# A GNN and attention kernel whose beginning was reordered: x loaded ahead of the weights, q of the first group by plain products, later norms and transposes among its products

## Chip, cores, metric

One core of a Trainium2 chip. The metric is the device time of one execution in microseconds (us), median of several. The profile's span, about 1.8 us shorter, is that of one profiled execution. The granted clock is TensorE's, as a share of its full speed, as the profile gives it.

## The reference

Input x is 128 batches of 128 rows of 512, float32. Layer 0 adds to each row one number from adj times the normed x. Layer 1 is masked attention with 8 heads.

```python
h = jnp.maximum(_layernorm(x, axis=-1), 0.0)
x = x + _L0_gnn_ref(h, adj, adj, L0_gnn_b)   # a row maximum of adj @ h + b, clipped at 0
h = jnp.maximum(_layernorm(x, axis=-1), 0.0)
q = (x @ Wq + bq); k = (x @ Wk + bk); v = (x @ Wv + bv)   # of this h
scores = einsum(q, k) / 8 + mask(adj == 0); weights = softmax(scores)
x = x + einsum(weights, v)
```

Layer 0 adds a constant per row, which the second norm takes out again. So both layers share one normed h, and the kernel norms each batch once.

## The kernel before

A group is four batches. For each batch: `norm` (statistics on VectorE, `rstd` on POOL), `norm_end` (h on VectorE, scaled on ScalarE; POOL adds bv to x for the output), transposes on TensorE (the first two groups only), and `adjacency` (TensorE product, maximum on VectorE). For each group and each of q, k, v there are seven fast products p1 to p7 (a Strassen scheme) of sums of h and of the weight, in place of eight. Cuts are marked with `...`.

```python
ps_mm = ctx.enter_context(tc.tile_pool(name="ps_mm", bufs=4, space=PSUM))
ps_sc = ctx.enter_context(tc.tile_pool(name="ps_sc", bufs=1, space=PSUM))
ps_av = ctx.enter_context(tc.tile_pool(name="ps_av", bufs=1, space=PSUM))
...
nc.scalar.dma_start(adj_sb, adj)
load(0)                                        # x of batches 0-3, two pieces, on SP's queue
for name, src in (("q", wq), ("k", wk), ("v", wv)):
    nc.scalar.dma_start(W[name], src.rearrange("(c p) f -> p c f", p=P))
nc.gpsimd.dma_start(b0_sb, ...)                # then bq, bk, bv on POOL's queue
...
def norm_end(m):
    g, i = divmod(m, G)
    nc.vector.tensor_scalar(HN[m], X[g][:, i, :], MV[m][:, 0:1], 0.0, op0=ALU.subtract, op1=ALU.max)
    nc.scalar.activation(HN[m], HN[m], AF.Copy, scale=RSTD[m])
    nc.gpsimd.tensor_tensor(X[g][:, i, :], X[g][:, i, :], bv_sb, op=ALU.add)
...
for g in (0, 1):
    for m in range(g * G, g * G + G + 1):
        if m < g * G + G:
            norm(m); norm_end(m)
        if m > g * G:
            transposes(m - 1); adjacency(m - 1)
    for k in range(4):
        h_sum(g, k)                            # VectorE
    if g == 0:
        weight_sums(nc.vector, "q"); weight_sums(nc.gpsimd, "k"); weight_sums(nc.gpsimd, "v")
        PR[0] = q, k, v = [Products(0, n) for n in "qkv"]
        for p in (q.p1, q.p6, q.p2, ..., v.p5, v.p4):
            p()
for m in (2 * G, 2 * G + 1):
    norm(m); norm_end(m); blocks(m); adjacency(m)
...
for b in range(B):                             # the loop: scores, products of the next group, output
    ...
```

The instructions are issued on each engine in the order written.

## Time and profile before

| | before |
|---|---|
| median time | 1646.46 us (1645.5 to 1647.39, 4 runs) |
| span of the profiled run | 1643.9 us |
| TensorE, VectorE, ScalarE, POOL busy | 97%, 68%, 26%, 16% |
| first scores (start of the loop) | 95.51 us |
| from there to the end | 1548.4 us |

I call the start of the first scores T. It is the first TensorE instruction that writes the tile `sc` from `qT` and `kT` in the timeline. From there TensorE has no gap until its last batches.

### The profile page before, as it was taken

To read this page: it belongs to the slowest core of one execution; us is meant where nothing else is said; L and a number is where in the kernel's file an instruction comes from. 1 tells how busy PE (TensorE), PEld (TensorE's weight loads), DVE (VectorE), ACT (ScalarE), POOL (GpSimd) and SP (SyncE) were. 2 spreads that over 40 slices of the span, in tenths; PEclk is the share of its full clock that TensorE was granted. 3 is DMA by queue.
4 is the path that set the end of the run, shared out by engine and by line. 5 is a ranking of instruction groups with operands and counts; after the bars stand their busy time and mean duration, and the time that the engine had idled before them with its cause. 6 is when DMAs were issued, how large, how long until landed. Compare 5 with 4: busy or idle time off the path is not lost.

```text
span 1643.9 us, 29453 instructions
## 1 busy us (share of the span) xinstructions
PE 1593.4 (97%) x11811; PEld 1326.5 (81%) x11811; DVE 1124.6 (68%) x2050; ACT 421.3 (26%) x841; POOL 262.4 (16%) x278
## 2 busy tenths in 40 slices
PE   4879999999999999999999999999999999999996
PEld 3658888888888888888888888888888888888885
DVE  5467676677776677776677777677777677777655
ACT  2222222222222222222222222222222222222221
POOL 5111111111111111111111111111111111111000
PEclk8989999999999999999999999999999999999998
DMA  4022223322223322223322223322223322123201
GB/s 161 1 49 49 65 66 77 69 68 48 62 71 73 69 69 50 61 71 71 71 68 54 56 70 71 70 69 65 45 69 71 72 69 67 42 69 72 52 20 40
DMA packets 299003, 104.02 MB, mean 63 GB/s; under 512 B 264369, under 2 KB 264497, under 8 KB 298865
## 3 DMA queue, kind: packets, MB, share of 16 engines
q1 hardware_dynamic: 296960, 98.64, 24.9%
q10 hardware_dynamic: 1728, 3.21, 0.6%
q8 instruction: 94, 1.54, 0.4%
q0 software_dynamic: 176, 0.27, 0.1%
q14 instruction: 45, 0.36, 0.1%
HBM read 37.03 MB, written 33.55 MB: 43 GB/s over the span
## 4 chain that ended last, share of the span: by engine, by line
PE 94%; issue 3%; DVE 1%; POOL 1%; ACT 0%; DMA 0%; DVEq 0%; POOLq 0%
PE mm L357 70%; PE sc L442 9%; PE pav L464 9%; PE mm L298 7%; DMA xg<-in_x_dram 0%; DVE w L455 0%; POOL rstd L257 0%; DVE st L252 0%; PE mm L292 0%; ACT hn L265 0%; DVE amax L299 0%; DVE hs L316 0%; POOL xg L266 0%; POOL sk_sb L325 0%; POOL sv_sb L323 0%
## 5 line engine op out<-in xcount | busy, mean ns | idle before, releaser
L257 POOL TENSOR_TENSOR rstd<-ve,mhalf 128x1 f32<-128x1 f32 x128 | 84.6, 661 | 1246.3 <-DVE ve L255 1216.7
L450 ACT ACTIVATE w<-sc 128x512 f32<-128x512 f32 x256 | 138.9, 595 | 518.3 <-PE sc L442 518.3
L464 PEld LDWEIGHTS pav<-v,w 128*64 128x64 f32 x4096 | 131.1, 138 | 99.9 <-issue 54.8
L357 PE MATMUL mm<-hs,sq_sb 128*128 128x256 f32 x768 | 186.2, 386 | 8.9 <-DVE sq_sb L324 8.9
L357 PE MATMUL mm<-sv_sb,hs 128*128 128x256 f32 x768 | 176.3, 379 | 0.0
L357 PE MATMUL mm<-hs,sk_sb 128*128 128x256 f32 x768 | 176.2, 379 | 0.0
L357 PEld LDWEIGHTS mm<-hs,sq_sb 128*128 128x128 f32 x768 | 144.6, 192 | 31.3 <-issue 9.2
L266 POOL TENSOR_TENSOR xg<-xg,bv_sb 128x512 f32<-128x512 f32 x128 | 162.7, 1271 | 33.4 <-DVE hn L262 26.9
L455 DVE TENSOR_TENSOR w<-w,live 128x512 f32<-128x512 f32 x256 | 164.7, 685 | 3.2 <-ACT w L450 3.2
L265 ACT ACTIVATE hn<-hn,rstd 128x512 f32<-128x512 f32 x128 | 92.9, 725 | 273.5 <-DVE hn L262 202.3
L357 PEld LDWEIGHTS mm<-sv_sb,hs 128*128 128x128 f32 x768 | 146.2, 190 | 19.6
L357 PEld LDWEIGHTS mm<-hs,sk_sb 128*128 128x128 f32 x768 | 146.2, 190 | 19.6
L464 PE MATMUL pav<-v,w 128*64 128x65 f32 x4096 | 149.4, 225 | 6.9 <-DVE w L455 6.9
L442 PE MATMUL sc<-qT,kT 64*128 64x128 f32 x2048 | 151.1, 288 | 0.0
L298 PE MATMUL mm<-hn,adjT 128*128 128x512 f32 x256 | 137.0, 618 | 9.6 <-ACT hn L265 9.6
L405 DVE TENSOR_TENSOR u<-mm,p1b 128x512 f32<-128x512 f32 x64 | 44.3, 692 | 132.4 <-PE mm L357 132.4
L442 PEld LDWEIGHTS sc<-qT,kT 64*128 64x128 f32 x2048 | 126.4, 190 | 10.3 <-issue 1.5
L357 PE MATMUL mm<-hT,wk_sb 128*128 128x256 f32 x512 | 124.2, 386 | 0.0
L357 PE MATMUL mm<-hT,wq_sb 128*128 128x256 f32 x512 | 124.2, 386 | 0.0
L299 DVE TENSOR_REDUCE amax<-mm 128x1 f32<-128x512 f32 x128 | 86.1, 673 | 54.7 <-PE mm L298 54.1
L357 PE MATMUL mm<-wv_sb,hT 128*128 128x256 f32 x512 | 121.0, 379 | 0.0
L357 PEld LDWEIGHTS mm<-wv_sb,hT 128*128 128x128 f32 x512 | 97.5, 190 | 13.0
(81 smaller groups left out, 2026.8 us busy)
## 6 DMA issues: line engine op xcount, KB each, us to landing
xg<-in_x_dram SPq DMA_DIRECT2D x64, 512.0 KB, 5.2
out_dram<-o SPq DMA_DIRECT2D x128, 256.0 KB, 2.1
hT<-tb SPq DMA_DIRECT2D x960, 32.0 KB, 2.0
wq_sb<-in_L_gnn_Wq_dram ACTq DMA_DIRECT2D x1, 1024.0 KB, 11.4
wk_sb<-in_L_gnn_Wk_dram ACTq DMA_DIRECT2D x1, 1024.0 KB, 16.2
wv_sb<-in_L_gnn_Wv_dram ACTq DMA_DIRECT2D x1, 1024.0 KB, 18.6
bv_sb<-in_L_gnn_bv_dram POOLq DMA_DIRECT2D x1, 256.0 KB, 8.7
adj_sb<-in_adj_dram ACTq DMA_DIRECT2D x1, 64.0 KB, 3.3
```

Of the source, the lines that this page charges most:

```text
L257: nc.gpsimd.tensor_tensor(rstd, ve, mhalf, op=ALU.pow)
L265: nc.scalar.activation(HN[m], HN[m], AF.Copy, scale=RSTD[m])
L266: nc.gpsimd.tensor_tensor(X[g][:, i, :], X[g][:, i, :], bv_sb, op=ALU.add)
L298: nc.tensor.matmul(pa, adjT, HN[m], start=True, stop=True)
L299: nc.vector.reduce_max(AMAX[g][:, i : i + 1], pa, axis=AX.X)
L357: nc.tensor.matmul(bank[:, r, :], lhs, rhs, start=first and r == 0 and c == 0, stop=r == 1 and c == 1, skip_group_check=True,)
L405: nc.vector.tensor_tensor(self.u3, self.b, self.pf[1], op=ALU.add)
L442: nc.tensor.matmul(psc[:, j, f, :], KT[g][r, f, i * D : (i + 1) * D], QT[g][r, f, i * D : (i + 1) * D], start=True, stop=True,)
L450: nc.scalar.activation(w[:, j], psc[:, j], AF.Exp, scale=HD ** -0.5)
L455: nc.vector.tensor_tensor(w[:, j], w[:, j], live_h, op=ALU.mult)
L464: nc.tensor.matmul(pav[r, h // 4, (h % 4) * HE : (h % 4 + 1) * HE], w[:, h % 2, h // 2, r], V[g % 2][:, i, h, :], start=True, stop=True,)
```

## The change

The intent: let TensorE start earlier and keep it fed until the loop. (1) x comes ahead of the weights, over two queues. (2) q of group 0 by plain products, which need no sums; VectorE makes the sums of k meanwhile, and POOL those of v (those of q, for the later groups, follow among the products). (3) Norms, transposes and adjacency of batches 4 to 9 stand among the products of k and v. Transposes now use the buffer of the scores and early adjacency that of the output, each of which exists once, and one small copy goes from VectorE to ScalarE.

```diff
-        load(0)
+        X[0] = xpool.tile([P, G, N], F32, name="xg")
+        for i in range(G):
+            (nc.sync, nc.scalar)[i % 2].dma_start(X[0][:, i, :], x[i])
         for name, src in (("q", wq), ("k", wk), ("v", wv)):
-            nc.scalar.dma_start(W[name], src.rearrange("(c p) f -> p c f", p=P))
+            for h in range(2):
+                (nc.sync, nc.scalar)[h].dma_start(W[name][:, 2 * h : 2 * h + 2, :], ...)
...
+        def plain_q(t):
...
+            for f in range(2):
+                bank = ps_mm.tile([P, 2, HT2], F32, name="mm")
+                for r in range(2):
+                    k = 2 * f + r
+                    for c in range(NC):
+                        nc.tensor.matmul(bank[:, r, :], W["q"][:, c, k * P : (k + 1) * P], h[:, :, c], ...)
+                    nc.scalar.activation(QT[0][:, k, ...], bank[:, r], AF.Identity, bias=bq_sb[:, k : k + 1])
...
+            for m in range(G):
+                norm(m)
+                norm_end(m)
+                if m > 0:
+                    early(m - 1)            # transposes and adjacency
+            plain_q(0)
+            early(G - 1)
+            weight_sums(nc.vector, "k")
+            for k in range(4):
+                h_sum(0, k)
+            plain_q(1)
+            weight_sums(nc.gpsimd, "v")
+            for s, p in enumerate((k.p1, k.p6, k.p2, k.p7, k.p5, k.p4, v.p1, k.p3, v.p6, v.p2, v.p7, v.p5, v.p4)):
+                p()
+                m = G + s // 2
+                if m < 2 * G + 2:
+                    if s % 2 == 0:
+                        norm(m)
+                        norm_end(m)
+                    elif m < 2 * G:
+                        early(m)
+                    else:
+                        blocks(m)
+                        adjacency(m, ...)
...
```

More of the change, by code (lines that the diff above doesn't have):

```diff
@@ L219, in fast @@
         nc.scalar.dma_start(adj_sb, adj)
-        load(0)
+        X[0] = xpool.tile([P, G, N], F32, name="xg")
+        for i in range(G):
+            (nc.sync, nc.scalar)[i % 2].dma_start(X[0][:, i, :], x[i])
         for name, src in (("q", wq), ("k", wk), ("v", wv)):
-            nc.scalar.dma_start(W[name], src.rearrange("(c p) f -> p c f", p=P))
+            for h in range(2):
+                (nc.sync, nc.scalar)[h].dma_start(
+                    W[name][:, 2 * h : 2 * h + 2, :],
+                    src[2 * h * P : (2 * h + 2) * P].rearrange("(c p) f -> p c f", p=P),
+                )
         nc.gpsimd.dma_start(b0_sb, b0.rearrange("(p o) -> p o", o=1))
@@ L237, in fast @@
         nc.tensor.transpose(pt[:, :D], adj_sb, ident)
-        nc.vector.tensor_copy(adjT, pt[:, :D])
+        nc.scalar.copy(adjT, pt[:, :D])
         nc.vector.tensor_single_scalar(live, adjT, 0.0, op=ALU.not_equal)
@@ L289, in transposes, with adjacency @@
             g, i = divmod(m, G)
-            ph = ps_mm.tile([P, NC, D], F32, name="mm")
+            ph = ps_sc.tile([P, 2, NC, D], F32, name="sc")
             for c in range(NC):
-                nc.tensor.transpose(ph[:, c], HN[m][:, c * P : (c + 1) * P], ident)
-            nc.scalar.copy(HT[g][:, i], ph)
-        def adjacency(m):
+                nc.tensor.transpose(ph[:, 0, c], HN[m][:, c * P : (c + 1) * P], ident)
+            nc.scalar.copy(HT[g][:, i], ph[:, 0])
+        def adjacency(m, pa=None):
             g, i = divmod(m, G)
-            pa = ps_mm.tile([P, 512], F32, name="mm")
+            if pa is None:
+                pa = ps_mm.tile([P, 512], F32, name="mm")
             nc.tensor.matmul(pa, adjT, HN[m], start=True, stop=True)
@@ L316, in h_sum, with weight_sum @@
             nc.vector.tensor_sub(HB[g][o], HB[g][a], HB[g][b])
-        def weight_sums(eng, n):
-            w = W[n]
-            a11, a21 = w[:, 0:2, 0:HT2], w[:, 0:2, HT2:N]
-            a12, a22 = w[:, 2:4, 0:HT2], w[:, 2:4, HT2:N]
-            s1, s2, s3, s4 = (WS[n][:, k] for k in range(4))
-            eng.tensor_tensor(s1, a21, a22, op=ALU.add)
-            eng.tensor_tensor(s2, s1, a11, op=ALU.subtract)
-            eng.tensor_tensor(s3, a11, a21, op=ALU.subtract)
-            eng.tensor_tensor(s4, a12, s2, op=ALU.subtract)
-            WA[n] = dict(a11=a11, a12=a12, a22=a22, s1=s1, s2=s2, s3=s3, s4=s4)
+        def weight_sum(eng, n, k):
+            if k == 0:
+                w = W[n]
+                WA[n] = dict(
+                    a11=w[:, 0:2, 0:HT2], a21=w[:, 0:2, HT2:N],
+                    a12=w[:, 2:4, 0:HT2], a22=w[:, 2:4, HT2:N],
+                    **{f"s{j + 1}": WS[n][:, j] for j in range(4)},
+                )
+            o, a, op, b = ("s1 a21 + a22", "s2 s1 - a11", "s3 a11 - a21", "s4 a12 - s2")[k].split()
+            eng.tensor_tensor(
+                WA[n][o], WA[n][a], WA[n][b], op=ALU.add if op == "+" else ALU.subtract
+            )
+        def weight_sums(eng, n):
+            for k in range(4):
+                weight_sum(eng, n, k)
         class Products:
@@ L418, in p3 @@
                 self.add(self.dst(0, 1), self.c, self.u2)
+        def plain_q(t):
+            if t == 0:
+                QT[0] = proj.tile([P, NC, T], F32, name="qT")
+            h = HT[0][:, 2 * t : 2 * t + 2]
+            for f in range(2):
[3 more added lines that the diff above has]
+                    for c in range(NC):
+                        nc.tensor.matmul(
+                            bank[:, r, :], W["q"][:, c, k * P : (k + 1) * P], h[:, :, c],
+                            start=r == 0 and c == 0, stop=r == 1 and c == NC - 1,
+                            skip_group_check=True,
+                        )
+                    nc.scalar.activation(
+                        QT[0][:, k, t * HT2 : (t + 1) * HT2], bank[:, r], AF.Identity,
+                        bias=bq_sb[:, k : k + 1],
+                    )
         def products(g):
@@ L482, in fast, with early @@
         with tc.manual_schedule():
-            for g in (0, 1):
-                for m in range(g * G, g * G + G + 1):
-                    if m < g * G + G:
+            def early(m):
+                transposes(m)
+                adjacency(m, ps_av.tile([P, 2, 512], F32, name="pav")[:, 0])
+            for m in range(G):
[6 more added lines that the diff above has]
+            weight_sums(nc.vector, "k")
+            for k in range(4):
+                h_sum(0, k)
+            plain_q(1)
+            weight_sums(nc.gpsimd, "v")
+            _, k, v = PR[0] = [None] + [Products(0, n) for n in "kv"]
+            for s, p in enumerate((
+                k.p1, k.p6, k.p2, k.p7, k.p5, k.p4, v.p1, k.p3, v.p6, v.p2, v.p7, v.p5, v.p4,
+            )):
+                p()
+                m = G + s // 2
+                if m < 2 * G + 2:
+                    if s % 2 == 0:
                         norm(m)
                         norm_end(m)
-                    if m > g * G:
-                        transposes(m - 1)
-                        adjacency(m - 1)
-                for k in range(4):
-                    h_sum(g, k)
-                if g == 0:
-                    weight_sums(nc.vector, "q")
-                    weight_sums(nc.gpsimd, "k")
-                    weight_sums(nc.gpsimd, "v")
-                    PR[0] = q, k, v = [Products(0, n) for n in "qkv"]
-                    for p in (
-                        q.p1, q.p6, q.p2, q.p7, q.p5, q.p4, k.p1, k.p6, q.p3, k.p2, k.p7,
-                        k.p5, k.p4, v.p1, k.p3, v.p6, v.p2, v.p7, v.p5, v.p4,
-                    ):
-                        p()
-            for m in (2 * G, 2 * G + 1):
-                norm(m)
-                norm_end(m)
-                blocks(m)
-                adjacency(m)
+                    elif m < 2 * G:
+                        early(m)
+                    else:
+                        blocks(m)
+                        adjacency(m, ps_av.tile([P, 2, 512], F32, name="pav")[:, 0])
+                if s >= 4 and s % 2 == 0 and s < 12:
+                    weight_sum(nc.gpsimd, "q", s // 2 - 2)
+                if s >= 8 and s < 12:
+                    h_sum(1, s - 8)
             move(2 * G + 1)
```

## The prediction

> **What bounds the kernel now.** I read the page's busy shares and slices first, then the busy times by stretch, then the timeline of the first 100 us engine by engine, then the chain of waits there. TensorE is busy 97% of the span, and the slice row is full from the seventh slice on. What the page calls low is the beginning, and the change touches only that.
>
> ```profile
> PE   4879999999999999999999999999999999999996
> PEclk8989999999999999999999999999999999999998
> ```
>
> A slice is 41 us, so some 30 to 40 us of TensorE time are missing in the first 100 us, besides the end, which the change leaves alone. The stretches tell where (columns: length, busy us of PE, PEld, DVE, ACT, POOL with counts, granted clock, DMA share, GB/s):
>
> ```profile
> 8.40:21.50 13.10, 8.04 (x23) 4.13 (x24) 4.94 (x12) 4.04 (x8) 7.18 (x8) 0.87 0.98 352
> 21.50:32.90 11.40, 2.55 (x11) 1.57 (x9) 10.45 (x9) 2.13 (x5) 11.24 (x8) 0.84 0.01 3
> 32.90:65.40 32.50, 32.50 (x144) 28.40 (x145) 10.41 (x14) 4.42 (x10) 0.96 (x1) 0.95 0.00 1
> 65.40:95.50 30.10, 15.02 (x38) 7.04 (x36) 17.41 (x38) 6.34 (x10) 11.44 (x12) 0.69 0.00 1
> ```
>
> There are two holes. From 21.5 to 32.9 TensorE waits for VectorE, which makes the operand sums of the first fast product. From 65.4 to 95.5 it waits for the norms of batches 4 to 9, at a mean clock of 0.69. The timeline has the instructions (start, us, engine, line, idle before and its releaser):
>
> ```profile
> 12.30 1.26 POOL L266 TENSOR_TENSOR xg<-xg,bv_sb 128x512 f32<-128x512 f32 x1 [5.14 <-issue]
> 13.52 0.73 POOL L257 TENSOR_TENSOR rstd<-ve,mhalf 128x1 f32<-128x1 f32 x1
> 20.01 0.72 ACT L265 ACTIVATE hn<-hn,rstd 128x512 f32<-128x512 f32 x1 [2.79 <-POOL rstd L257]
> 22.14 1.89 PE L357 MATMUL mm<-hT,wq_sb 128*128 128x256 f32 x8
> 32.88 3.53 PE L357 MATMUL mm<-hs,sq_sb 128*128 128x256 f32 x8 [8.85 <-DVE sq_sb L324]
> 43.16 1.89 PE L357 MATMUL mm<-hT,wk_sb 128*128 128x256 f32 x8
> 93.50 2.07 PE L298 MATMUL mm<-hn,adjT 128*128 128x512 f32 x2 [3.42 <-ACT hn L265]
> 95.51 2.08 PE L442 MATMUL sc<-qT,kT 64*128 64x128 f32 x16
> ```
>
> At 95.51 the loop over batches begins and TensorE then runs without gaps at about 11 us a batch. So the change is worth the shift of that one time. I call it T; it is 95.5 now.
>
> **What the Trainium skill says.** (1) "TensorE: Matmul & The Clock Gate", Part 1: the array runs at half rate until it has been busy for a window of about 3.4 us. The trace agrees: the eight instructions at 32.88, after 8.85 us of idleness, take 3.53 us, the same eight at 43.16 take 1.89. (2) The same page, under engine queue depths: ACT, DVE and GpSimd run strictly in order. The trace agrees: rstd of batch 1 on POOL waits behind the addition of bv to batch 0, and that addition waits for bv, which landed 8.7 us after its issue at 3.50, so at 12.2. (3) "DMA: Bandwidth & Descriptors", Issuing engines are not separate DMA queues: transfers from all issuers interleave on the same 16 engines. The trace agrees: share 0.98 at 352 GB/s with two queues active, so splitting x over two queues adds no bandwidth. (4) "SBUF — State Buffer", SBUF: two separate sides: a VectorE instruction with two inputs in SBUF and a GpSimd one that reads it exclude each other. The trace agrees: a 128x512 sum on VectorE takes 0.68 us alone, but starts at 1.64 to 1.75 us intervals while POOL makes weight sums, and POOL's go from 1.27 to 1.7.
>
> **Part one: x first.** x of batch 0 lands some 1 us earlier than the 5.22 us of now (256 KB on each of two queues in place of 512 KB beside a weight). It buys nothing: POOL holds rstd of batch 1 until bv is there. Transfers from POOL's queue take turns with the two others, as before; smaller pieces of x ahead of it may bring bv earlier by up to 2 us. I take 0.5 us.
>
> **Part two: the first four batches.** Transposes go to a buffer that exists once (of the scores) and adjacency to another (of the output), where four were free before. So transposes of batch 1 wait for the copy of batch 0, which stands behind hn of batch 1 on ACT: 14.3 + 0.7 + 0.5 = 15.5 in place of 15.06. Adjacency of batch 2 waits for amax of batch 1. Cost about 0.5 us, which cancels the gain of part one. So hn of batch 3 is at about 20.5, transposes and adjacency of batch 2 end at about 20.
>
> **Part three: q by plain products.** Each half is 16 products of 128x256, which the trace will show as 32 instructions (the 4 that make up one fast product show as x8). A fast product starts every 1.727 us (mean of 43.16 to 60.42, ten of them), so a half is 4 x 1.727 = 6.9 us and both are 13.8. Seven fast products of q took 12.1, so this is 1.7 us more TensorE work. But the first half starts at 20 with no sums, and the second follows batch 3's transposes and adjacency (1.36 us, from 20.78 to 22.14): 20.0 + 6.9 + 1.4 + 6.9 = 35.2. During it VectorE makes 4 k sums and 4 h sums from about 29 on. POOL's v sums start at 21.2 and need about 4 x 1.3 us, so they are over; VectorE needs 8 x 0.65 = 5.2 us and is ready at 34.5. The hole of 21.5 to 32.9 is gone.
>
> **Part four: norms among the products.** From 35.2 on: 13 products x 1.727 = 22.5 us, four pairs of transposes and adjacency x 1.36 = 5.4, two adjacencies x 0.86 (the steady loop, 106.42 to 107.28) = 1.7. Sum 29.6, end 64.8 if no gap is left. There are gaps. The order of instructions shows each batch's norm on VectorE behind amax of the batch before it, and in three of six steps (6, 8, 9) also behind a sum that reads a product just finished. From the end of what VectorE reads, TensorE waits for: [the sum 0.7 +] statistics 0.7 + mean 0.2 + ve 0.2, rstd on POOL 0.7, hn on ACT 0.7, with 0.02 to 0.1 between engines. Worked through by step:
> - batch 4: hn stands on ACT behind the four bias copies of the first product (1.5 us): gap 0.75
> - batches 5 and 7: chain from adjacency to hn 3.45 us, beside two products of 3.45: gap 0 to 0.1 each
> - batches 6, 8, 9: sum, norm, rstd, hn from the end of the first product of the step is 0.2 + 3.2, beside one product of 1.73: gap 1.7 each
> Together 0.75 + 0.1 + 3 x 1.7 = 5.95 us. T = 64.8 + 5.9 = 70.7.
>
> **The sum.** 95.5 - 70.7 = 24.8. The first scores also no longer start cold: 16 instructions took 2.01 us on the chain where a later batch took 1.09, so 0.9 more. 25.7 us, or 1.56% of 1646.0: 1620.3. I predict 1620.
>
> **Rivals.**
> - *The gaps among the products are not there* (VectorE and ACT run ahead further than I think). Then T is 65 and the time 1614. For: DVE is busy only 10.4 of 32.5 us beside the products now. Against: its instructions run in order, and the sums stand ahead of the norms.
> - *The early chain moves too*: bv lands at 9, hn of batch 3 comes 3 us earlier, and the time is 1617. With the first rival 1611, the only way I see to more than 2%. For: the transfers ahead of bv are smaller. Against: the engines are as full as before, and stats of batch 2 wait for amax of batch 0 at 11.4 anyway.
> - *New waits*: single buffers and gaps push TensorE under the busy share that keeps its clock up, so products among the norms run at half rate in part. Stretch 65.4 to 95.5 shows 0.69 at half occupancy. If 20% of 30 us ran at half rate, 3 to 6 us would be lost: 1624 to 1627. Against: TensorE would be some 80% busy here (24 of 30 us), where it was half idle then.
> - *Nothing moves, since some engine other than TensorE bounds the loop*: against it, TensorE has no idle time after 96 us.
>
> **Range and chances.** The gaps are sized from four steps, with 0.5 us of doubt each, the early chain by 2 us, the clock by 3: low 1614.5, high 1626. Over 2% faster needs 1613.1 or less, that is T under 62.6, which is below the gapless 64.8 and needs an earlier bv besides: 0.07. Slower by 2% would need T above 128: 0.01.
>
> **What would show it.** In the changed kernel: the first scores at 69 to 72 us; plain products dense from 20 to 35 but for one pair of transposes and adjacency; hn of batch 1 still after bv, at 12 to 14.5; between the k and v products idle time of TensorE released by hn of ACT, 1.5 to 2 us before batches 6, 8 and 9 and under 1 before 4; granted clock above 0.9 from 25 us on; the loop from T to the end as long as before, within 2 us. I would be wrong if x or weights came later than their users, if the plain products ran at half rate, or if the loop itself got longer.

## The result, and the profile after

| | before | after |
|---|---|---|
| median time | 1646.46 us | 1622.02 us (1621.72 to 1622.17, 4 runs) |
| ratio | 1 | 0.9851, 95% interval 0.9834 to 0.9868 |
| span of the profiled run | 1643.9 us | 1620.0 us |
| first scores, T | 95.51 us | 74.97 us |
| from T to the end | 1548.4 us | 1545.0 us |

The change won 24.4 us, 1.5%. Of the 23.9 us in the spans, T gives 20.5 and the loop 3.4.

The page's slices after, TensorE busy share and granted clock in tenths, one digit for 40.5 us:

```profile
PE   6899999999999999999999999999999999999996
PEclk9999999999999999999999999999999999999999
```

Two slices below nine are left at the beginning where there were three. The stretches of the changed kernel, cut at the first plain product, the first k product and the first scores (same columns as in the prediction):

```profile
0.00:20.05 20.05, 8.01 (x19) 4.17 (x20) 7.84 (x19) 4.59 (x7) 9.39 (x21) 1.00 0.89 312
20.05:38.58 18.53, 16.27 (x72) 12.52 (x71) 8.13 (x16) 5.05 (x10) 8.18 (x8) 1.00 0.06 21
38.58:74.97 36.39, 30.70 (x133) 22.92 (x131) 20.20 (x41) 10.47 (x19) 15.19 (x15) 1.00 0.00 1
```

The stretch of the norms, half idle before, is now 84% busy (30.70 of 36.39). The timeline after, the lines that answer to those of before:

```profile
12.11 1.26 POOL L273 TENSOR_TENSOR xg<-xg,bv_sb 128x512 f32<-128x512 f32 x1 [6.42 <-DVE mv L260]
13.33 0.73 POOL L264 TENSOR_TENSOR rstd<-ve,mhalf 128x1 f32<-128x1 f32 x1
20.05 1.89 PE L445 MATMUL mm<-hT,wq_sb 128*128 128x256 f32 x8
22.51 3.72 PE L445 MATMUL mm<-hT,wq_sb 128*128 128x256 f32 x16 [0.56 <-ACT qT L450]
26.79 1.99 PE L445 MATMUL mm<-hT,wq_sb 128*128 128x256 f32 x8 [0.56 <-ACT qT L450]
...
42.73 0.65 PE L299 MATMUL sc<-ident,hn 128*128 128x128 f32 x4 [0.54 <-ACT hn L272]
54.26 0.66 PE L299 MATMUL sc<-ident,hn 128*128 128x128 f32 x4 [1.69 <-ACT hn L272]
65.92 1.13 PE L306 MATMUL pav<-hn,adjT 128*128 128x512 f32 x2 [1.76 <-ACT hn L272]
72.19 1.12 PE L306 MATMUL pav<-hn,adjT 128*128 128x512 f32 x2 [1.69 <-ACT hn L272]
74.97 1.16 PE L477 MATMUL sc<-qT,kT 64*128 64x128 f32 x16
```

POOL's wait is where it was: the addition of bv starts at 12.11, though the page names another releaser (the statistics of batch 2, at about the same time); bv was issued at 3.50 and took 8.5 us to land. The predicted gaps ahead of batches 4, 6, 8 and 9 are there, at 0.54, 1.69, 1.76 and 1.69 us. What the prediction lacked is the wait inside the plain products. Their results go to a bank (one tile of `ps_mm`, in two halves of 256 columns), from which ScalarE copies each half to `qT`. TensorE waits for these copies (lines 22.51 and 26.79, and twice more in the second half). From 20.05 to 22.51 are 2.46 us, where the eight instructions need 1.73.

The loop's 3.4 us have two parts. One, predicted, is that the first scores are warm: 1.09 us on the chain where they took 2.01. The other, 2.5 us, lies in the last batches. Timeline of before with the stretch of its slow scores (columns as above, the granted clock third from the end), then the scores of the same batches after:

```profile
1622.00 1.16 PE L442 MATMUL sc<-qT,kT 64*128 64x128 f32 x16
1626.50 1.97 PE L442 MATMUL sc<-qT,kT 64*128 64x128 f32 x16
1629.98 2.29 PE L464 MATMUL pav<-v,w 128*64 128x65 f32 x32 [1.51 <-DVE w L455]
1632.20 1.76 PE L442 MATMUL sc<-qT,kT 64*128 64x128 f32 x16
1626.50:1632.20 5.70, 4.17 (x52) 3.59 (x48) 2.94 (x5) 1.08 (x2) 0.00 (x0) 0.51 0.13 49
```

```profile
1600.54 1.16 PE L477 MATMUL sc<-qT,kT 64*128 64x128 f32 x16
1604.70 1.16 PE L477 MATMUL sc<-qT,kT 64*128 64x128 f32 x16
1608.86 1.16 PE L477 MATMUL sc<-qT,kT 64*128 64x128 f32 x16
```

There, in the profiled run of before, TensorE ran slower for two batches. The diff does not touch that code. So I took this for chance and tested it (e10). About 0.3 us of the 2.5 are not the clock: the batch ahead, from 1622.00 to 1626.50, took 4.50 us at a clock of 1.00, where it takes 4.16 after. e10 has these 4.50 us too; their cause is open.

### The profile page after: what moved, and what is told of

The parts are those of the page before. It is cut to its first block, busy times and chain, and to the rows that moved or that the text cites. A ratio compares the mean times of both kernels' runs of the same rounds, so it can differ in the third digit from the quotient of the medians.

```text
span 1620.0 us, 29469 instructions
## 1 busy us (share of the span) xinstructions
PE 1586.6 (98%) x11819; PEld 1319.8 (81%) x11819; DVE 1114.2 (69%) x2044; ACT 422.9 (26%) x844; POOL 259.6 (16%) x278
## 4 chain that ended last, share of the span: by engine, by line
PE 97%; DVE 1%; ACT 1%; issue 0%; DMA 0%; POOL 0%; ACTq 0%; DVEq 0%; POOLq 0%
PE mm L372 72%; PE pav L499 9%; PE sc L477 8%; PE mm L306 6%; PE mm L445 1%; PE pav L306 1%; PE sc L299 0%; DVE w L490 0%; DMA xg<-in_x_dram 0%; ACT hn L272 0%; DVE o L512 0%; DVE o L508 0%; POOL rstd L264 0%; DVE st L259 0%; ACT qT L450 0%
## 5 line engine op out<-in xcount | busy, mean ns | idle before, releaser
L372 PE MATMUL mm<-hs,sq_sb 128*128 128x256 f32 x744 | 179.0, 383 | 0.0
L372 PEld LDWEIGHTS mm<-hs,sq_sb 128*128 128x128 f32 x744 | 138.8, 190 | 21.4
L306 PE MATMUL mm<-hn,adjT 128*128 128x512 f32 x236 | 120.5, 592 | 0.0
L372 PE MATMUL mm<-hT,wq_sb 128*128 128x256 f32 x496 | 120.4, 386 | 0.0
L372 PEld LDWEIGHTS mm<-hT,wk_sb 128*128 128x128 f32 x512 | 94.7, 190 | 15.8 <-issue 0.5
```

What stands on the lines that cost most here:

```text
L306: nc.tensor.matmul(pa, adjT, HN[m], start=True, stop=True)
L372: nc.tensor.matmul(bank[:, r, :], lhs, rhs, start=first and r == 0 and c == 0, stop=r == 1 and c == 1, skip_group_check=True,)
```

## The experiments

Twelve kernels, each on one chip with the kernel before; all were correct. "Rest" is span minus T.

| run | T | rest | median | ratio to before, 95% interval |
|---|---|---|---|---|
| before | 95.51 | 1548.4 | 1646.46 | 1 |
| changed kernel | 74.97 | 1545.0 | 1622.02 | 0.9851 (0.9834 to 0.9868) |
| e1_q_acts_late | 71.95 | 1546.2 | 1619.31 | 0.9835 (0.9817 to 0.9853) |
| e2_norm_first | 70.48 | 1545.0 | 1619.25 | 0.9837 (0.9819 to 0.9855) |
| e3_old_loads | 73.60 | 1545.0 | 1621.95 | 0.9854 (0.9836 to 0.9872) |
| e4_bv_late | 70.50 | 1545.0 | 1619.23 | 0.9841 (0.9819 to 0.9862) |
| e5_q_fast | 82.56 | 1548.0 | 1632.88 | 0.9927 (0.9908 to 0.9945) |
| e6_norms_after | 90.90 | 1546.7 | 1639.87 | 0.9970 (0.9951 to 0.9989) |
| e7_all_three | 62.73 | 1546.5 | 1610.69 | 0.9790 (0.9771 to 0.9809) |
| e9_bv_late_old_loads | 73.25 | 1547.1 | 1619.23 | 0.9842 (0.9823 to 0.9860) |
| c1_after_again | 75.74 | 1545.0 | 1624.27 | 0.9875 (0.9860 to 0.9890) |
| e10_before_fill | 96.98 | 1546.4 | 1644.38 | 0.9993 (0.9980 to 1.0007) |
| e8_all_three_mm | 62.17 | 1546.4 | 1610.32 | 0.9787 (0.9773 to 0.9800) |
| e11_all_three_fill | 62.90 | 1547.5 | 1612.22 | 0.9803 (0.9789 to 0.9816) |

The changed kernel itself differed by 2.3 us between two chips (c1). So differences of medians under some 2 us decide nothing here, and T decides. T has its own spread: two profiles of the changed kernel give 74.97 and 75.74 (c1), and two of the same beginning before give 95.51 and 96.98 (e10). A shift of T under some 1.5 us therefore counts only where the lines show where it comes from.

T comes from one profile each, so e1, e2 and e4 should be checked against the other runs. By medians they win only 2.7 to 2.8 us, where T says 3.0, 4.5 and 4.5. All four runs of the changed kernel had a clock of 0.998 over the whole run. The runs of e2 and e4 at 0.998 took 1617.2 to 1617.3 us, 4.7 us less than its 1622.0, in agreement with T; their other runs, at 0.994 to 0.997, took 1619.2 to 1621.3.

### e5: q of group 0 by fast products again

```diff
-            plain_q(0)
             early(G - 1)
-            weight_sums(nc.vector, "k")  ...  plain_q(1); weight_sums(nc.gpsimd, "v")
+            (h sums; weight_sums of q on VectorE, of k and v on POOL)
+            for p in (q.p1, q.p6, q.p2, q.p7, q.p5, q.p4, q.p3):
+                p()
```

> The plain products of q undone alone: q of group 0 by seven fast products as in the kernel before, its sums on VectorE, those of k and v on POOL; new loads and norms among the k and v products kept. Theory (the plain products fill the wait for the sums): the hole of 9 us before the second product of q is back, k starts at 45 to 46 in place of 38.58, the first scores start 6.5 to 7.5 us later (about 82), time near 1629. Rival (they only trade waiting for more products, 13.8 us and 3.2 us of new waits against 12.1 us): the first scores start less than 2 us later.

T was 82.56, 7.6 us later, and the time 1632.9, 10.9 us longer (expected 1629); 3 us of that are a slow end (rest 1548.0). Timeline of e5:

```profile
33.61 3.78 PE L372 MATMUL mm<-hs,sq_sb 128*128 128x256 f32 x8 [8.28 <-DVE sq_sb L336]
82.56 1.16 PE L477 MATMUL sc<-qT,kT 64*128 64x128 f32 x16
```

The hole before the second product is back. The plain products are worth 7.6 us, with their own waits inside. A cheaper cure was not tried: in the kernel before, VectorE's sums start every 1.65 us beside POOL's weight sums (24.43 to 34.33), and without them every 0.64 us (after, 30.99 to 35.45). So holding POOL's sums back might have closed part of the hole too.

### e6: norms and transposes behind the products again

```diff
             for s, p in enumerate((k.p1, ..., v.p4)):
                 p()
-                (norms, early, blocks, adjacency and h sums of batches 4 to 9 by step)
+            (norms, early and h sums of batches 4 to 7, then norms, blocks, adjacency of 8 and 9)
```

> The placing of norms and transposes undone alone: the k and v products run without them, the norms of batches 4 to 9 come behind as in the kernel before; new loads and plain q kept. Theory (this part is worth most): k and v products end at about 61, then some 30 us at low clock as before (65.4 to 95.5), first scores at 91 to 92, time 1638 to 1640. Rival (the gaps among the products give most of it back): first scores below 84.

T was 90.90, 15.9 us later, the time 1639.9. About 1 us of it is not the edit's: adjacency of batch 2 ran at a lower rate and plain q began at 21.00. Stretch of e6 from the end of the products to the scores:

```profile
62.40:90.90 28.50, 13.43 (x29) 5.76 (x28) 16.73 (x37) 6.34 (x10) 11.42 (x12) 0.68 0.00 1
```

TensorE is half idle at a clock of 0.68, as in the kernel before. The placing of the norms is worth about 15 us, the largest part.

### e3: the old loads

```diff
-        (x of group 0 by batch on two queues, weights in halves on two queues)
+        load(0)
+        for name, src in (("q", wq), ("k", wk), ("v", wv)):
+            nc.scalar.dma_start(W[name], src.rearrange("(c p) f -> p c f", p=P))
```

> Only the loads undone: x on one queue in two pieces a group, each weight whole on the other queue, as in the kernel before; all else as changed. Theory (VectorE starts 1.4 us later, but POOL holds the second batch's rstd until bv lands at 12 us in either order): bv lands at 12.2 and the first scores start within 0.4 us of 74.97, the time stays within 0.6 us of 1622. Rival (the early x is what the first part gains by): the first scores start 1.4 us later or more.

T was 73.60: 1.4 us earlier than the changed kernel, against both theories. Plain q started as much earlier, at 18.68. First statistics started at 5.05 in place of 3.77, as expected, but bv landed at 11.0. POOL's lines in e3:

```profile
11.14 1.26 POOL L267 TENSOR_TENSOR xg<-xg,bv_sb 128x512 f32<-128x512 f32 x1 [4.17 <-issue]
12.36 0.55 POOL L258 TENSOR_TENSOR rstd<-ve,mhalf 128x1 f32<-128x1 f32 x1
```

Over the profiled runs, bv took 8.7, 7.5, 7.9 and 8.3 us with the old loads (before, e3, e9, e10) and 8.3 to 9.2 with the new ones. So x ahead of the weights won nothing here; if anything the new loads hold bv back by about half a microsecond. That is from one profile each, with overlap, and I do not call it shown.

### e4 and e9: POOL's additions out of the way

```diff
             nc.scalar.activation(HN[m], HN[m], AF.Copy, scale=RSTD[m])
-            nc.gpsimd.tensor_tensor(X[g][:, i, :], X[g][:, i, :], bv_sb, op=ALU.add)
+            if g > 0: (the addition)
...
+            for m in range(G): (the addition)
             plain_q(0)
```

> Only POOL's additions of bv to the first four batches moved behind the four rstd. Theory (POOL's order makes the early chain wait for bv): rstd of batch 1 runs at about 7 us in place of 13.3, hn of batch 3 ends at 16 to 17 in place of 21.5, plain q starts at 15 to 16 in place of 20.05 and the first scores start 4 to 5 us earlier, the time falls to about 1617.5. Rival (the single buffers and the weights landing at 12 to 13 us hold the chain anyway): less than 2 us is won.

T was 70.50, 4.5 us earlier. Timeline of e4:

```profile
6.35 0.72 POOL L264 TENSOR_TENSOR rstd<-ve,mhalf 128x1 f32<-128x1 f32 x1 [0.66 <-DVE ve L262]
15.66 1.89 PE L450 MATMUL mm<-hT,wq_sb 128*128 128x256 f32 x8
70.50 1.16 PE L482 MATMUL sc<-qT,kT 64*128 64x128 f32 x16
```

The second rstd runs at 6.35 in place of 13.33. So the addition of bv, which nothing needs before the output, held the beginning back by its place in POOL's order. e9 is e4 with the loads of e3:

> bv additions late as in e4, and the old loads as in e3: with POOL's wait for bv gone, the arrival of x should count. Theory (the early x is hidden behind bv's wait and shows once that is gone): first statistics at 5.1 in place of 3.8, first scores 1.0 to 1.5 us later than e4's 70.50, so 71.5 to 72. Rival (x is hidden by something else too, such as the second pair of batches waiting for amax): within 0.3 us of 70.50.

T was 73.25, 2.75 us later than e4, more than both theories allowed. Timeline of e9:

```profile
8.70 1.12 PE L298 MATMUL sc<-ident,hn 128*128 128x128 f32 x4 [3.39 <-ACT hn L266]
17.57 2.70 PE L444 MATMUL mm<-hT,wq_sb 128*128 128x256 f32 x8
73.25 1.16 PE L476 MATMUL sc<-qT,kT 64*128 64x128 f32 x16
```

The first transposes come 1.0 us later (8.70 against 7.67 in e4), and that is the gain of the early x. The rest is rate: adjacency of batch 2 took 1.92 us where e4 took 1.02, and the first plain product 2.70 where it took 1.89. So the early x is worth 1.0 us once POOL no longer waits. The granted clock from 16 to 20 us was 0.60 in e9 and 1.00 in e4. Whether the other 1.7 us belong to the later x or to chance, one profile cannot tell. In the medians nothing shows, as both are at 1619.23.

On the old loads, POOL's additions out of the way won only 0.35 us of T (73.60 in e3, 73.25 in e9); in e3 bv landed early (11.0), and in e9 the clock was low. In the medians it won 2.7 us there and 2.8 us on the new loads. So 4.5 us is the gain where bv lands at 12.0, and not a fixed one.

### e1: bias copies behind both halves of the bank

```diff
                     for c in range(NC):
                         nc.tensor.matmul(bank[:, r, :], ...)
-                    nc.scalar.activation(QT[0][:, k, ...], bank[:, r], ...)
+                for r in range(2):
+                    nc.scalar.activation(QT[0][:, 2 * f + r, ...], bank[:, r], ...)
```

> Only the plain products of q: the bias copies of a bank are issued after both its halves are written, not between them. Theory (the bank is the unit of waiting: TensorE may not write its second half while ScalarE reads its first): the four waits of 0.73 to 0.83 us within the plain products go, the first scores start 3.0 us earlier (at about 72.0 in place of 74.97) and the time falls by about 3 us, to 1619. Rival (the gaps are ScalarE being late for another reason, or come back as waits before the k products): the first scores move by less than 1 us.

T was 71.95, 3.0 us earlier. Timeline of e1, the two halves of q:

```profile
20.08 7.07 PE L445 MATMUL mm<-hT,wq_sb 128*128 128x256 f32 x32
28.55 7.17 PE L445 MATMUL mm<-hT,wq_sb 128*128 128x256 f32 x32
```

Each half is one unbroken stretch of 7.1 us. The first k product started at 35.56 in place of 38.58. So the four waits were TensorE waiting to write the second half of a bank until ScalarE had read the first.

### e2: the norm ahead of the product of its step

```diff
-                p()
                 m = G + s // 2
-                ... if s % 2 == 0: norm(m); norm_end(m)
+                if m < 2 * G + 2 and s % 2 == 0: norm(m); norm_end(m)
+                p()
```

> Only the order within a step: each norm is issued ahead of the product of its step, not behind it. Theory (gaps before batches 4, 6, 8, 9 are VectorE's and ScalarE's order: the norm stands behind a sum that reads a product just finished): gaps of 0.54, 1.69, 1.76, 1.69 fall to 0.3 or less each, the first scores start about 5 us earlier (near 70), the time falls by about 5 us, to 1617. Rival (the chain from one batch's adjacency to the next batch's hn is itself too long, whatever the order): gaps of about 1 us and more stay and less than 2.5 us is won.

T was 70.48, 4.5 us earlier (4.8 us counted from the first k product, which came 0.3 us later here). Timeline of e2, the four places of the gaps:

```profile
42.38 0.60 PE L299 MATMUL sc<-ident,hn 128*128 128x128 f32 x4
52.12 0.66 PE L299 MATMUL sc<-ident,hn 128*128 128x128 f32 x4
62.24 1.13 PE L306 MATMUL pav<-hn,adjT 128*128 128x512 f32 x2 [0.22 <-ACT hn L272]
67.70 1.13 PE L306 MATMUL pav<-hn,adjT 128*128 128x512 f32 x2 [0.88 <-ACT hn L272]
```

Three of the four gaps are gone or small, and the last is 0.88: short of the 0.3 expected. There VectorE still has the sums of group 1 and a block transpose ahead of the maximum and the norm. The order on VectorE and ScalarE was the cause of most of it.

### e7, e8: the three together

> The three gains together: bias copies of plain q behind both halves, norms ahead of their products, POOL's bv additions behind the four rstd. Theory (the three waits are in series): plain q starts at 15.7, the first k product at 31, the first scores at 62 to 64, 11 to 13 us earlier than the changed kernel, time 1609 to 1611, that is over 2% faster than the kernel before. Rival (one hides another: the k sums on VectorE or the loads of batches 4 and 5 become the wait): first scores at 66 or later.

e7 has the edits of e1, e2 and e4. T was 62.73, 12.2 us earlier than the changed kernel; 3.0 + 4.5 + 4.5 = 12.0, so they add up and none hides another. The time was 1610.7, ratio 0.979, so it beats both kernels. Whether it is over 2% faster than the kernel before, as expected, is unclear: the interval reaches 0.9809. Its stretches, cut as above:

```profile
0.00:15.76 15.76, 7.40 (x19) 3.67 (x20) 7.02 (x19) 4.56 (x7) 6.42 (x18) 1.00 0.85 289
15.76:31.25 15.49, 15.38 (x71) 12.85 (x70) 7.67 (x12) 4.19 (x9) 9.97 (x9) 1.00 0.37 134
31.25:62.73 31.48, 30.38 (x133) 23.00 (x131) 21.96 (x45) 10.65 (x20) 17.31 (x16) 1.00 0.00 1
```

From 15.76 on TensorE is busy all but 1.2 us. e8 also moves transposes and adjacency of the first four batches back to the pool of four buffers:

```diff
-            ph = ps_sc.tile([P, 2, NC, D], F32, name="sc")      # for g == 0
+            ph = ps_mm.tile([P, NC, D], F32, name="mm")
```

> The three gains of e7, and transposes and adjacency of the first four batches back in the pool of four buffers, as in the kernel before. Theory (single buffers cost some 0.5 us in the early chain, as predicted): transposes of batch 2 start at 13.9 in place of 14.4, the first scores at about 62.2 in place of 62.73. Rival (nothing, since hn of batch 2 arrives with the copy): within 0.2 us.

T was 62.17, 0.56 us earlier. That is less than T's spread, but the lines show where it comes from. Transposes of batch 2 start at 14.41 in e7, released by the copy `hT`, and at 13.85 in e8, released by `hn`; plain q follows at 15.76 and 15.20. So the single buffers cost some 0.5 us, as the prediction had it. In the median (1610.3) that is not to be seen.

### c1, e10, e11: the clock at the end

> The changed kernel again, unedited, on the chip of the next three, as their measure. Expected 1622 within 1 us, first scores at 75.0 within 0.5; runs spread over 1 to 4 us by the clock of the last batches.

c1, the changed kernel unedited on another chip: 1624.27 (1622.49 to 1625.81), T 75.74, later since bv took 9.2 us. Both missed what was expected. e10 puts work into the gaps of the last four batches of the kernel before:

```diff
+                if g == NG - 1:
+                    fill = ps_mm.tile([P, 512], F32, name="mm")
+                    for c in range(3):
+                        nc.tensor.matmul(fill[:, 0:HT2], W["q"][:, c, 0:P], W["q"][:, c, 0:HT2], start=c == 0, stop=c == 2)
                 finish(g, i, w)
```

> The kernel before, with three useless products (128x256, the result is not read) in each of the last four batches, between scores and output, where TensorE waits 1.5 us and more for the masks. Theory (the 2.5 us that the loop lost in the profile of before, and the spread of its runs, 1642 to 1649, come from the clock falling in the last batches, by chance of its phase): runs within 1 us of each other at 1643 to 1644, about 2 us below the median of before; scores of the last batches at 1.16 us in every case. Rival (the spread has another source): spread and median as before, or up to 1 us more.

Rest fell from 1548.4 to 1546.4, and all scores of the last batches took 1.16 us. The spread of its runs was 1.6 us, against 2.7 for before in the same rounds, and the median 0.9 us lower: less than the theory had for both. The slow end in the profile of before is the clock falling (0.51 from 1626.50 to 1632.20) where TensorE had been busy 2.46 of 4.50 us. That the filler removes it is not shown: of the twelve profiles without filler, five (after, e2, e3, e4, c1) have a fast end as well. And the end is not all of the spread: T itself varied (96.98 here, 95.51 in the first profile), and the ratio, 0.9993, does not tell the two kernels apart. e11 is e7 with this filler:

> The three gains of e7 and the filler of e10. Theory: runs within 1 us of each other at 1608 to 1609, about 2 us below e7. Rival: as e7, 1610.7 with a spread of 2 us.

It missed: 1612.2, slower than e7 by 1.5 us. The scores were all at 1.16 us, yet the span went on for 5.3 us after the last counted instruction, in place of 2.8. The profile shows why in the register and branch instructions, which the page does not count. The program ends with a branch (`tc.If`, to a general path that is not taken). On TensorE's sequencer (PEldq) it took, in ns, first in e11 and then in e7:

```profile
L617 PEldq COMPARE_BRANCH  x1: 3548/3548/3548, 1605.8 to 1605.8; - x1
L610 PEldq COMPARE_BRANCH  x1: 361/361/361, 1607.0 to 1607.0; - x1
```

In all other thirteen profiles it took 0.36 to 0.37 us. After the last counted instruction, e11 has two transfers of the queue that loads instructions (q8), e7 one; whether the branch waits for them is not shown. Without these 2.5 us e11's rest would be 1545.0, that of a fast end. So as it stands the filler is no gain, and in this profile the loss is at the branch, not in the last batches. Why the branch was slow stays open.

## Why the prediction held, step by step

The prediction was 1620, and 1622.0 came. The mechanism was right but for one wait, which the prediction lacks; so two terms of the sum were off, in opposite directions.

- **x first is worth nothing.** Right in the result (e3). The reason given, POOL's wait for bv, is shown by e4 and e9. "Smaller pieces of x ahead of it may bring bv earlier" was wrong: bv landed at 12.0, not 11.7.
- **Single buffers cost about 0.5 us.** Right: 0.56 (e8 against e7, on e7's chain). Plain q started at 20.05, predicted 20.
- **"A half is 4 x 1.727 = 6.9 us."** This is the step that failed. From the first plain product to the first k product it took 18.5 us in place of 15.2. I priced TensorE's work and left out that ScalarE reads each bank while TensorE still has to write its other half. e1 shows it: 3.0 us. VectorE's sums, expected to be ready at 34.5, were ready at 36.1, which held nothing up. The Trainium skill would have told me: "PSUM — Partial Sum Buffer", PSUM bank collisions raise a hardware error, says that two engines must not use one bank and quadrant at once, even at different columns, and that waits are to be set by bank. The trace agrees: four waits, 0.73 to 0.83 us each from start to start.
- **Gaps of 0.75, 0.1 and three times 1.7 us.** Measured 0.54, under 0.15, and 1.69, 1.76, 1.69. Right, and its cause is shown by e2. From k to the scores it took 36.4 us, predicted 35.5. The gaps as starts show them, 1.85 to 1.92 us, were a little longer than their idle part.
- **The loop as long as before, less 0.9 us for warm scores.** Measured 3.4. Of the further 2.5 us some 2.2 come from the clock at the end of the profiled run of before, which I had read as part of the loop, and 0.3 from a wait there that stays open. This hid most of the 4.3 us that T came late.
- **Rivals.** Gaps that are not there: false for the changed kernel, true of e2. bv landing earlier: it did not, but taking its wait away gives 4.5 us. The clock falling among the norms: it did not; it was 1.00 from 20 us to T. Nothing moves: false, T moved by 20.5 us.
- **Slips that cost nothing.** The row of slices is full from the fourth slice on, not the seventh. The "1.64 to 1.75 us intervals" of VectorE's sums are their durations; they start 1.55 to 1.78 us apart. Over 2% faster needs T under 63.5 by the prediction's own sum, not 62.6: the 0.9 us of warm scores was left out there.

So that 1622 lies within 2 us of 1620 is in part luck: T came 4.3 us late and the rest was 2.5 us shorter than predicted.

## What to carry to other kernels

Price a block of products with the engine that empties its bank: issue all products of a bank before the first read of it, or TensorE waits inside the block. On an engine that works in order, put what the next stage needs ahead of what waits for a product just issued or for a late load; that was worth some 9 us of T here in two edits of a few lines (e2, e4). Read the start of the loop from the timeline when runs spread more than the effect.

## What the Trainium skill lacked or had wrong

- "TensorE: Matmul & The Clock Gate", HAM oscillation: its rule is to leave no TensorE gap above about 3.4 us. In the last batches the gaps are at most 1.9 us and TensorE is busy 2.46 of 4.50 us; there the clock fell all the same in some profiles (scores at 1.97 us in place of 1.16). Gaps of 1.7 us in a stretch that is 84% busy did no harm. The page does say further on that frequent short idles can bring the clock down, but gives no busy share, which would be needed beside the gap.
- "SBUF — State Buffer", SBUF: two separate sides: of VectorE and POOL, the second to start is said to block fully. With both making 128x512 sums, VectorE's started every 1.65 us. Alone, VectorE's start every 0.64 us and POOL's every 1.26, together 1.90. So some 0.25 us of each pair seem to overlap (POOL's spans are rough).
- "PSUM — Partial Sum Buffer": right about the bank as unit of waiting, but without what such a wait costs: here 0.73 to 0.83 us for each read of half a bank.
- No page says how long a small load by POOL's queue takes beside two full queues: 256 KB took 7.5 to 9.2 us, and 0.5 KB 5.5 to 6.3 us.
